# Depthwise 7x7 filter as band-matrix products: blocks of 4 full-width rows become blocks of 7 half-width rows

## The chip, the cores and the metric

The kernel runs on one core of a Trainium2 chip. The metric is the device time of one execution in microseconds (us); lower is better. The kernel before takes 3096.03 us (median of 3 runs, 3095.71 to 3096.39). PE is the matrix engine (its weight loads are shown as PEld), DVE the vector engine, ACT the scalar engine, POOL the general engine, SP the engine that issues most DMAs.

## What is computed

A batch of 32 images of 384 channels and 28 x 28 pixels goes through one ConvNeXt block and a gate. Cut to what matters:

```
y = conv(x, dw_w, padding 3, feature_group_count=C) + dw_b    # 7x7, one filter per channel
y = (y - mean_c) * rsqrt(var_c + eps) * ln_g + ln_b            # over the channels
y = gelu(y @ w1 + b1)                                          # 384 -> 1536
y = grn_g * (y * gx / (mean(gx) + eps)) + grn_b + y            # gx = norm over the pixels
z = x + (y @ w2 + b2)                                          # 1536 -> 384
out = sigmoid(logits(mean, max, min of z) + z)
```

The change bears on the first line. All data are fp32.

## The kernel before

There are two stages. The first, some 0.5 ms, computes the depthwise filter for all images, channel by channel; the second runs image by image through the two large products (`up` and `down`), each computed with fewer block products by a scheme of sums (`UPSTEPS`, `STEPS`, `SUMS`).

**The filter as matrix products.** An image is cut into NJ = 7 blocks of RW = 4 rows. A row is padded to a pitch PW = 32, so that a block is a vector of 4 x 32 = 128 numbers, which lie on the 128 partitions. Each channel has a band matrix (each column is the filter's weights, shifted by one). A block of the output is the sum of three products: the block itself, the block after and the block before, each with another 128 (or 96) columns of the band matrix. All blocks of all 32 images stand side by side as moving columns: 7 x 32 = 224 for the block itself (L599), 6 x 32 = 192 for each neighbour (L601, L603), since the outermost blocks have one neighbour only. So a channel has three products. A product in fp32 appears in the profile as two records, one for each of two passes; a transpose has one.

**The steps.** `for s in range(NK)` has 48 steps of TC = 8 channels. `conv(s, c2, ...)` does two channels into one PSUM tile `pc` (four tiles rotate), and the result, with the bias, is copied into `yc`: even pairs by two ACT activations (L615), odd pairs by one DVE addition (L607). `yc` holds 16 channels for all images; `store` sends it to DRAM (`yd`, and the last two groups to `yl`).

**Band matrices.** `sequences(cb)` puts the 49 weights of a channel into a row of zeros of FL = 355 numbers, which is written to DRAM (`fs`). `load_t(s)` reads a step's matrices back into `tmat` with one DMA, in which every partition reads the same row shifted by one number (128 partitions, 11,360 bytes each). It is issued three steps ahead.

**The input.** `load_x` fetches a tile of XC = 32 channels by 4 images (128 partitions, 784 pixels). `pad_x` copies it into the pitch of 32 (`xpad`, three rotate; POOL for the first chunk of 32 channels, ACT after that, L448). `turn_x` transposes it on PE, block by block, in two halves of 4 and 3 blocks (L460, seven transposes a tile), and copies the result into `xt` (DVE, L469). `spread` deals this work for the next chunk out among the pairs of the current one: `plan` sets behind which pair each half tile goes, and `pad_next(i + 1)` stands ahead of the first half of tile i. PE executes in the written order (`keep`).

**SP's queue** carries, in written order: `load_t`, `load_x`, the stores of `yc`, and the stores of the combined weight blocks `u` that POOL forms meanwhile (`form_w`).

**The end of the first stage.** The last 16 channels are done twice with half of the images each (`B0 = 16`): first images 0 to 15, then 16 to 31. With the first half done, image 0 has all its channels, and `first_image` (normalisation, transposes back to channel order, sums of `forms_up`) is dealt out among the pairs of the second half. Then `up(0)` begins.

**The second stage.** For each image `load_y` fetches the filter's result, DVE computes statistics per block (`block_stats`), ACT normalises per block (`norm`, 384 numbers a pixel), PE transposes three times per block (`turn`, L816), ACT copies into `room` and leaves the padding out (`untwist`, called by `evac`), and POOL forms the sums. Where these stand among the products is written by hand in `within` and `beside`. There are 7 blocks an image, hence 21 transposes.

Of the kernel before, what the change touches and what calls it, by code (L numbers as in the profile page):

```python
# [21 lines left out]
RH = HW // 2  # L22
# [7 lines left out]
RW = 4  # L30
NJ = HW // RW
PW = P // RW
XC = 32
# [3 lines left out]
REACH = 3 * PW  # L37
MW = P + 2 * REACH
T0 = P - REACH

SN = 6 * PW + 7
S0 = T0 + REACH + P - 1 - 3 * PW - 3
FL = S0 + SN
NLAST = XC // YC
# [149 lines left out]
def convnext_gate_kernel(  # L196
# [15 lines left out]
    N = NJ * B  # L212
# [5 lines left out]
    fs = [dram.tile([P + 1, FL], F32, name=f"fs_{cb}") for cb in range(CB)]  # L218
# [60 lines left out]
    def stats(b):  # L279

        mv = sts[b] = smp.tile([P, NJ, 2], F32, tag="mv", name=f"mv_{b}")
        if b == 0:
            bs = bss[0].rearrange("p j i v -> p j (i v)")
        else:
            bs = bss.pop(b)
        for j in range(NJ):
            nc.vector.bn_aggr(mv[:, j, :], bs[:, j, :])
# [6 lines left out]
    def std(b):  # L294
        mv = sts[b]
        sd = smp.tile([P, NJ], F32, tag="sd", name=f"sd_{b}")
        nc.scalar.activation(sd, mv[:, :, 1], AF.Sqrt, bias=eps_t, scale=1.0)
        rstd = smp.tile([P, NJ], F32, tag="rstd", name=f"rstd_{b}")
        nc.vector.reciprocal(rstd, sd)
        nmr = smp.tile([P, NJ], F32, tag="nmr", name=f"nmr_{b}")  # L300
        nc.vector.scalar_tensor_tensor(nmr, mv[:, :, 0], -1.0, rstd, ALU.mult, ALU.mult)
        sts[b] = rstd, nmr
# [7 lines left out]
    def untwist(eng, acc, cb, j0, j1, pt):  # L310

        affine(
            eng,
            acc[:, cb, j0 * RW * HW : j1 * RW * HW].rearrange("p (r w) -> p r w", w=HW),
            pt[:, : j1 - j0, ::-1].rearrange("p j (r w) -> p j r w", w=PW)[:, :, :, :HW],
            lng_t[:, cb : cb + 1],
            lnb_t[:, cb : cb + 1],
        )
# [28 lines left out]
    with ExitStack() as one:  # L347
# [28 lines left out]
        tab = ws[:, : CB * FL].rearrange("p (cb m) -> p cb m", m=FL)  # L376
# [10 lines left out]
        nc.vector.memset(tab, 0.0)  # L387

        def sequences(cb):
            nc.vector.tensor_copy(  # L390
                tab[:, cb, S0 : S0 + SN - 7].rearrange("p (y x) -> p y x", x=PW)[:, :, :7],
                dww[:, cb, :42].rearrange("p (y x) -> p y x", x=7),
            )
            nc.vector.tensor_copy(tab[:, cb, S0 + SN - 7 :], dww[:, cb, 42:])
            return nc.scalar.dma_start(fs[cb][:P, :], tab[:, cb, :])

        sequences(0)
        zrow = scratch([FL], 1)
# [3 lines left out]
        def load_t(s, parts=1):  # L402
            base = fs[s * TC // P]
            n = TC // parts
            for i in range(parts):
                nc.sync.dma_start(
                    tmat[s % NT2][:, i * n : (i + 1) * n, :].rearrange("p c m -> p (c m)"),
                    bass.AP(
                        tensor=base.tensor,
                        offset=base.offset + (s * TC % P + i * n) * FL,  # L410
                        ap=[[1, P], [1, n * FL]],
                    ),
                )
# [3 lines left out]
        xpad = [tp.tile([P, HW, PW], F32, name=f"xpad_{i}") for i in range(NPAD)]  # L417
        for t in xpad:
            nc.gpsimd.memset(t[:, :, HW:], 0.0)
# [21 lines left out]

        def pad_x(i):
            dst = xpad[i % NPAD][:, :, :HW]
            src = xis.pop(i).rearrange("p (r w) -> p r w", w=HW)
            if i < NG:
                nc.gpsimd.tensor_copy(dst, src)
            else:
                nc.scalar.activation(dst, src, AF.Identity)  # L448
# [3 lines left out]
        def turn_x(i, h, xt, eng=nc.vector):  # L452

            g = i % NG
            xv = xt.rearrange("p c (j b) -> p j c b", j=NJ)
            j0, j1 = 4 * h, min(NJ, 4 * h + 4)
            pt = psx.tile([P, 4, P], F32, tag="pt", name=f"pt_{i}_{h}")
            for j in range(j0, j1):
                keep(
                    nc.tensor.transpose(  # L460
                        pt[:, j - j0, :],
                        xpad[i % NPAD][:, j * RW : (j + 1) * RW, :].rearrange("p r w -> p (r w)"),
# [3 lines left out]
            dst = xv[:, j0:j1, :, g * NB : (g + 1) * NB]  # L466
            src = pt[:, : j1 - j0, :].rearrange("p j (c q) -> p j c q", q=NB)
            if eng is nc.vector:
                eng.tensor_copy(dst, src)  # L469
            else:  # L470
                eng.activation(dst, src, AF.Identity)  # L471
# [57 lines left out]
        AHEAD = NG  # L529

        def pad_next(i):
            if i < GT:
                pad_x(i)
                if i + AHEAD < GT:
                    load_x(i + AHEAD)

        for i in range(AHEAD):
            load_x(i)
        xt = new_xt(0)
        for i in range(NG):  # L540
# [4 lines left out]
            if i == NG - 2:  # L545
                for cb in range(CB):
                    if cb:
                        keep(sequences(cb))
                    keep(nc.scalar.dma_start(fs[cb][P:, :], zrow))
            if i == NG - 2:  # L550

                nc.gpsimd.tensor_copy(tmat[1][:, 0, :1], xpad[i % NPAD][:, 0, :1])
                load_t(1)
            if i + AHEAD < GT:
                load_x(i + AHEAD)
            for h in range(2):
                turn_x(i, h, xt, (nc.vector, nc.scalar)[h])
        pad_next(NG)

        later = {  # L560
# [4 lines left out]
            U2 - 3: (  # L565
                ws.rearrange("p (fb c) -> p fb c", c=C),
                w2.rearrange("(fb p) c -> p fb c", p=P),
            ),
# [9 lines left out]
        B0 = min(B, 16)  # L578

        def conv(s, c2, yc, xt, b0, b1):  # L580

            t = tmat[s % NT2]
            nb = b1 - b0
            if not nb:
                return
            pc = psc.tile([P, 2, 256], F32, tag="pc", name=f"pc_{s}_{c2}_{b0}")
            for ci in range(2):
                c = 2 * c2 + ci
                if nb == B:
                    po = pc[:, ci, :N]  # L590
                    xc = xt[:, s % SK * TC + c, :]
                    after, before = xc[:, B:], xc[:, : N - B]
                    lo, hi = po[:REACH, : N - B], po[:, B:]
                else:
                    po = pc[:, ci, : NJ * nb].rearrange("p (j b) -> p j b", b=nb)
                    xc = xt[:, s % SK * TC + c, :].rearrange("p (j b) -> p j b", b=B)[:, :, b0:b1]
                    after, before = xc[:, 1:], xc[:, : NJ - 1]
                    lo, hi = po[:REACH, : NJ - 1], po[:, 1:]
                keep(nc.tensor.matmul(po, t[:, c, P : 2 * P], xc, start=True, stop=False))  # L599
                keep(  # L600
                    nc.tensor.matmul(lo, t[:, c, 2 * P : T0 + MW], after, start=False, stop=False)  # L601
                )
                keep(nc.tensor.matmul(hi, t[:, c, :P], before, start=False, stop=True))  # L603
            cc = s * TC + 2 * c2
            cy = cc % YC
            if c2 % 2:
                nc.vector.tensor_tensor(  # L607
                    yc[:, b0:b1, :, cy : cy + 2].rearrange("p b j c -> p c j b"),
                    pc[:, :, : NJ * nb].rearrange("p c (j b) -> p c j b", j=NJ),
                    dwb[:, cc : cc + 2].unsqueeze(2).unsqueeze(3).to_broadcast([P, 2, NJ, nb]),  # L610
                    ALU.add,
                )
            else:
                for ci in range(2):
                    nc.scalar.activation(  # L615
                        yc[:, b0:b1, :, cy + ci].rearrange("p b j -> p j b"),
                        pc[:, ci, : NJ * nb].rearrange("p (j b) -> p j b", j=NJ),
# [5 lines left out]
        def store(yc, kt, b0, b1):  # L623
# [6 lines left out]
            if b0 == 0:  # L630
                for j in range(NJ):
                    nc.vector.bn_stats(bss[0][:, j, 2 + i, :], yc[:, 0, j, :])
                nc.vector.tensor_copy(yis[0][:, kt], yc[:, 0])
            (nc.sync if b1 < B or i + 1 < NLAST else nc.scalar).dma_start(
                yl[:, i, b0:b1], yv[:, b0:b1]
            )
# [16 lines left out]
        def first_image(n):  # L653

            V, A = nc.vector, nc.scalar
# [12 lines left out]
            elif n in (2, 3):  # L668
                h = n - 2
                j0, j1 = 4 * h, min(NJ, 4 * h + 4)  # L670
# [10 lines left out]
                for cb in range(CB):  # L681
                    untwist((A, V, A)[cb], room_acc, cb, j0, j1, py[cb])
# [3 lines left out]
        for s in range(NK):  # L686
            k, si = divmod(s, SK)
            if s + 3 < NK:
                if s == 0:
                    for i in range(2, 4):  # L690
                        nc.gpsimd.tensor_copy(tmat[i][:, 0, :1], xpad[i % NPAD][:, 0, :1])
# [17 lines left out]
            if s >= NK - 2:  # L709


                if s == NK - 1:
                    for n in range(2 * PAIRS):
                        conv(NK - 2 + n // PAIRS, n % PAIRS, yc, xt, 0, B0)
                    store(yc, kt, 0, B0)
                    for i in range(0, NS, UG):
                        for t in range(2):
                            first_u1[t, i] = load_u1(t, i)
                    for n in range(2 * PAIRS):
                        conv(NK - 2 + n // PAIRS, n % PAIRS, yc, xt, B0, B)  # L720
                        first_image(n)
                    if B0 < B:
                        store(yc, kt, B0, B)
            else:
                for c2 in range(PAIRS):
                    conv(s, c2, yc, xt, 0, B)
                    if k + 1 < NX:
                        spread(k + 1, si * PAIRS + c2, xn)
                if s % 2:
                    store(yc, kt, 0, B)  # L730

                    for h, (k0, k1) in enumerate(((0, NY - NLAST - 4), (NY - NLAST - 4, NY - NLAST))):
                        if kt != k1 - 1:
# [476 lines left out]
```

## Time and profile before

| what | us |
|---|---|
| median of the runs | 3096.03 |
| time of the profiled execution | 3095.95 |
| its span, first to last instruction | 3094.2 |
| first product of the filter starts | 20.46 |
| last step with all images together ends | 471.9 |
| first product of `up(0)` starts | 496.04 |
| transposes of the input, L460 | 672, of which 56 ahead of the first product |
| transposes back in the second stage, L816 | 31 images x 21 |

The profile is of one execution. "Busy" is the time in which an engine had at least one instruction under way; matmuls overlap one another, so the mean duration of a record is longer than the time from one start to the next. In a list of instructions, "x2" means that two records were merged into one line; a duration is then that of both together. In the chain of waits each line gives start, duration and the instruction that the end of the run goes back to. A group line gives busy time, mean duration of one and the idle time of the engine just before it, with what ended it.

### The profile page before, as it was taken

Reading aid. Unit: us, or ns where it says so; the run is one execution under the profiler, and the core shown is the slowest. Engines: PE = TensorE matmul, PEld = TensorE weight load, DVE = VectorE, ACT = ScalarE, POOL = GpSimd, SP = SyncE. Lnnn points to the kernel's source line nnn. Section 1 sums busy time; section 2 is a strip of 40 time slices with the busy share of each in tenths; the row PEclk is TensorE's granted clock in tenths of the full one; section 3 lists DMA queues with packets and bytes.
Section 4 is the critical chain, followed back from the end, with each engine's and each line's share of the span. In section 5 each row is a group of like instructions: output and inputs, shape, how many; then the busy total and the mean of one; then the engine's idle time right before and its main releaser. Section 6 shows DMA issues by size and latency. Waiting matters only on the chain.

```text
span 3094.2 us, 45727 instructions
## 1 busy us (share of the span) xinstructions
PE 3059.3 (99%) x15011; PEld 2486.7 (80%) x15011; DVE 1986.1 (64%) x5378; ACT 1986.7 (64%) x3151; POOL 2263.1 (73%) x1767
## 2 busy tenths in 40 slices
PE   8999999999999999999999999999999999999997
PEld 8999997777777777777777777777777777777777
DVE  3444446666667777776667667666666666666665
ACT  3333335757777777777777777777777777777771
POOL 1233442798888888888888888888888888888887
PEclk9999999999999999999999999999999999999999
DMA  9999987455555655556656565655556555555545
GB/s 369 362 373 350 355 326 230 138 157 190 190 189 191 190 190 190 191 191 192 197 189 197 189 197 190 196 193 187 185 182 197 183 182 186 187 190 190 190 152 188
DMA packets 316132, 658.31 MB, mean 213 GB/s; under 512 B 127583, under 2 KB 142202, under 8 KB 306938
## 3 DMA queue, kind: packets, MB, share of 16 engines
q1 hardware_dynamic: 302916, 616.59, 60.2%
q10 hardware_dynamic: 12982, 38.80, 3.2%
q8 instruction: 122, 2.00, 0.3%
q14 instruction: 112, 0.92, 0.1%
HBM read 560.78 MB, written 94.53 MB: 212 GB/s over the span
## 4 chain that ended last, share of the span: by engine, by line
PE 95%; POOL 3%; ACT 1%; DVE 1%; DMA 1%; issue 0%; ACTq 0%; SPq 0%; POOLq 0%; DVEq 0%
PE ph_A L858 13%; PE ph_C L858 13%; PE ph_B L858 13%; PE pz_A L980 8%; PE pz_C L980 8%; PE pz_D L980 7%; PE pz_F L980 7%; PE pc L599 5%; PE pc L603 4%; PE pc L601 4%; PE py L816 2%; PE pt L460 2%; PE pz_H L980 2%; PE pz_E L980 2%; PE pz_I L980 2%; POOL d_room L941 1%
## 5 line engine op out<-in xcount | busy, mean ns | idle before, releaser
L941 POOL TENSOR_TENSOR d_room<-y 128x588 f32<-128x588 f32 x257 | 368.2, 1439 | 342.4 <-PE pz_B L980 194.0
L308 ACT ACTIVATE y<-y,fv,gsc 128x784 f32<-128x784 f32 x376 | 362.8, 1031 | 378.6 <-DVE gsc L894 378.6
L828 ACT ACTIVATE y<-y,fv 128x784 f32<-128x784 f32 x384 | 350.1, 945 | 186.4 <-DVE y L873 164.4
L858 PE MATMUL ph_A<-room,ws 128*128 128x392 f32 x1240 | 461.3, 494 | 0.8 <-ACT te L865 0.4
L858 PE MATMUL ph_C<-room,ws 128*128 128x392 f32 x1240 | 462.0, 495 | 0.0
L858 PE MATMUL ph_B<-room,ws 128*128 128x392 f32 x1240 | 458.8, 492 | 1.3 <-DVE yc L607 1.3
L941 POOL TENSOR_TENSOR d_room<-d_room,y 128x588 f32<-128x588 f32 x309 | 442.5, 1436 | 16.8
L858 PEld LDWEIGHTS ph_C<-room,ws 128*128 128x128 f32 x1240 | 233.1, 190 | 179.6 <-DVE y L871 20.6
L858 PEld LDWEIGHTS ph_A<-room,ws 128*128 128x128 f32 x1240 | 233.1, 190 | 178.7 <-ACT te L865 13.3
L858 PEld LDWEIGHTS ph_B<-room,ws 128*128 128x128 f32 x1240 | 234.8, 190 | 164.7 <-issue 1.5
L941 POOL TENSOR_TENSOR d_room<-y,d_room 128x588 f32<-128x588 f32 x220 | 316.0, 1437 | 46.0 <-PE pz_A L980 18.2
L834 ACT ACTIVATE junk<-y 128x784 f32<-128x784 f32 x384 | 329.0, 857 | 8.1
L343 POOL TENSOR_TENSOR room<-room 128x392 f32<-128x392 f32 x300 | 300.4, 1018 | 11.8
L941 POOL TENSOR_TENSOR y<-y 128x588 f32<-128x588 f32 x188 | 269.7, 1435 | 7.3
L867 DVE TENSOR_TENSOR y<-y,ph_C 128x392 f32<-128x392 f32 x384 | 214.3, 559 | 27.4
L1002 DVE TENSOR_REDUCE stq<-x 128x1 f32<-128x196 f32 x768 | 228.2, 349 | 5.5
L869 DVE TENSOR_TENSOR y<-y,ph_B 128x392 f32<-128x392 f32 x256 | 137.4, 557 | 143.5 <-ACT y L828 119.4
L615 ACT ACTIVATE yc<-pc,dwb 128x224 f32<-128x224 f32 (+1 forms) x200 | 103.5, 619 | 192.6 <-PE pc L603 184.1
L599 PE MATMUL pc<-xt,tmat 128*128 128x224 f32 (+1 forms) x800 | 213.9, 349 | 5.6 <-ACT xt L471 4.1
L980 PE MATMUL pz_A<-d_room,u 128*128 128x196 f32 x1056 | 204.9, 330 | 0.0
L524 POOL TENSOR_SCALAR u<-ws 128x384 f32<-128x384 f32 (+1 forms) x53 | 66.5, 1259 | 186.7 <-DMA u2d<-u 133.8
L469 DVE COPY xt<-pt 128x512 f32<-128x512 f32 (+1 forms) x184 | 112.1, 619 | 135.0 <-PE pt L460 135.0
(219 smaller groups left out, 6619.2 us busy)
## 6 DMA issues: line engine op xcount, KB each, us to landing
u<-u2d SPq DMA_DIRECT2D x487, 384.0 KB, 3.4
ws<-u1d SPq DMA_DIRECT2D x384, 320.0 KB, 3.0
tmat<-fs SPq DMA_DIRECT2D x47, 1420.0 KB, 11.4
ws<-u2d SPq DMA_DIRECT2D x121, 384.0 KB, 3.2
yd<-yc SPq DMA_DIRECT2D x22, 1792.0 KB, 6.6
yi<-yd SPq DMA_DIRECT2D x31, 1232.0 KB, 8.0
x<-in_x SPq DMA_DIRECT2D x32, 1176.0 KB, 5.4
out<-x ACTq DMA_DIRECT2D x31, 1176.0 KB, 7.2
```

The costliest lines, as they stand in the source:

```text
L308: eng.activation(out, in_, AF.Identity, bias=add, scale=mul)
L343: tc.keep_in_program_order(eng.tensor_tensor(d, o[in0], o[in1], op))
L599: keep(nc.tensor.matmul(po, t[:, c, P : 2 * P], xc, start=True, stop=False))
L601: nc.tensor.matmul(lo, t[:, c, 2 * P : T0 + MW], after, start=False, stop=False)
L828: nc.scalar.activation(y, y, AF.Gelu, bias=b1_t[:, f : f + 1], scale=1.0)
L834: nc.scalar.activation(junk, ys[b][:, f, :], AF.Square, accum_out=ssqs[b][:, f : f + 1])
L858: nc.tensor.matmul(banks[t, bk][:, :NH], wts[t][:, i % UG, :], o[opnd], start=(first == 1), stop=True, skip_group_check=True,)
L867: nc.vector.tensor_tensor(d, d, p, ALU.add)
L869: nc.vector.tensor_tensor(d, d, p, ALU.subtract)
L941: nc.gpsimd.tensor_tensor(d[0], o[a][0], o[c][0], ALU.add if sign == "+" else ALU.subtract)
L980: nc.tensor.matmul(pz[:, :NQ4], wt[:, i % UD, t, :], o[opnd][0][:, t, :], start=(first and t == 0), stop=(t == KD - 1), skip_group_check=True,
L1002: nc.vector.tensor_reduce(stq[:, v, m, h : h + 1], xh, AX.X, op2)
```

## The change

The blocks become 7 rows high and half as wide. The output of a block has 7 x 14 pixels in a pitch of PR = 19 (the last row is not padded, so 6 x 19 + 14 = 128 output partitions). The input blocks have 7 rows and KW = 18 columns (14, 3 of a neighbour and 1 over), 126 partitions, with the row index fastest, and are offset by 3 rows against the output: an output block needs two input blocks, the one above (`up_`) and the one below (`down_`). There are NV = 4 output blocks and NI = 5 input blocks per half, so NJ = 8 blocks an image, and per channel two halves x two products, all with 128 weight columns and 4 x 32 = 128 moving columns.

- A chunk has XC = 16 channels (two steps of 8) by 8 images instead of 32 by 4; there are still 96 tiles, now with eight transposes each.
- `pad_x` has four copies instead of one, since it also turns row and column over; the fifth block is made of three rows at the end and four at the start, and `turn_x` puts it to both ends with a mask (`ends`): three copies a half tile instead of one.
- FL is 268 instead of 355. `fs` has three variants per channel (all weights; first column alone; last column alone, for the outermost input columns), and `load_t` has three DMAs: 112 partitions, 7 and 7.
- The split of the last 16 channels is gone. `first_image` stands behind the last product, behind 36 transposes of the identity (`NWARM`) that no one reads.
- In the second stage an image has 8 blocks: 24 transposes, 8 normalisations and statistics. `yd` grows by 8/7. Several small tiles have two buffers instead of three. The load of `w2` is in two halves.

The core of the diff:

```diff
-RW = 4
-NJ = HW // RW
-PW = P // RW
-XC = 32
+RW = 7
+OW = HW // 2
+KW = OW + 4
+PR = OW + 5
+KP = RW * KW
+NV = HW // RW
+NJ = 2 * NV
+NI = NV + 1
+XC = 16
...
-                keep(nc.tensor.matmul(po, t[:, c, P : 2 * P], xc, start=True, stop=False))
-                keep(
-                    nc.tensor.matmul(lo, t[:, c, 2 * P : T0 + MW], after, start=False, stop=False)
-                )
-                keep(nc.tensor.matmul(hi, t[:, c, :P], before, start=False, stop=True))
+                for h, up_, down_ in ((0, UP_L, DOWN_L), (1, UP_R, DOWN_R)):
+                    po = pc[:, ci, h * NV * B : (h + 1) * NV * B]
+                    xc = xt[:KP, s % SK * TC + c, h * NI * B : (h + 1) * NI * B]
+                    for n, (m0, j) in enumerate(((up_, 1), (down_, 0))):
+                        keep(
+                            nc.tensor.matmul(
+                                po, t[:KP, c, m0 : m0 + P], xc[:, j * B : (j + NV) * B],
+                                start=(n == 0), stop=(n == 1),
+                            )
+                        )
...
+                for v, e0, ne in ((0, 1, KW - 2), (1, 0, 1), (2, KW - 1, 1)):
+                    nc.sync.dma_start(
+                        t[e0 * RW : (e0 + ne) * RW],
+                        bass.AP(
+                            tensor=base.tensor,
+                            offset=start + v * (P + 1) * FL + e0,
+                            ap=[[1, ne], [PR, RW], [1, n * FL]],
+                        ),
+                    )
...
+            d, x0 = xpad[i % NPAD], xis.pop(i)
+            xw = x0.rearrange("p (r w) -> p w r", w=HW)
+            for h, e0, c0 in ((0, 1, 0), (1, 0, HW - KW + 1)):
+                dst = d[:, h, : NV - 1, e0 : e0 + KW - 1, :]
+                src = xw[:, c0 : c0 + KW - 1, RW - 3 : HW - 3]
+                copy((A, V, G)[h + 1 if i < NG else 0], dst, src.rearrange("p w (j r) -> p j w r", r=RW))
...
+            copies = [(xv[:, 1:NV], src[:, : NV - 1], None)]
+            for v, j in enumerate((NV, 0)):
+                copies.append((xv[:, j], src[:, NV - 1], ends[:KP, v : v + 1]))
...
-                if s == NK - 1:
-                    for n in range(2 * PAIRS):
-                        conv(NK - 2 + n // PAIRS, n % PAIRS, yc, xt, 0, B0)
-                    store(yc, kt, 0, B0)
...
-                    for n in range(2 * PAIRS):
-                        conv(NK - 2 + n // PAIRS, n % PAIRS, yc, xt, B0, B)
-                        first_image(n)
...
+            if s == NK - 1:
...
+                for n in range(NWARM):
+                    pw = psx.tile([P, 4, P], F32, tag="pt", name=f"pw_{n}")
+                    for j in range(4):
+                        keep(nc.tensor.transpose(pw[:, j, :], ident, ident))
+                for n in range(4):
+                    first_image(n)
...
-            for i, jj in ((0, (0, 1)), (3, (2, 3)), (7, (4, 5)), (TURNED, (6,))):
+            for i, jj in ((0, (0, 1)), (3, (2, 3)), (7, (4, 5)), (TURNED, (6, 7))):
```

## The prediction

> **What bounds the kernel.** I read the page first, then the busy times by stage, the groups of the filter stage with shapes kept apart, the instructions of PEld, and the chain of waits at the seam of the two stages.
>
> ```profile
> PE 3059.3 (99%) x15011; PEld 2486.7 (80%) x15011; DVE 1986.1 (64%) x5378; ACT 1986.7 (64%) x3151; POOL 2263.1 (73%) x1767
> ...
> PE 95%; POOL 3%; ACT 1%; DVE 1%; DMA 1%; issue 0%; ACTq 0%; SPq 0%; POOLq 0%; DVEq 0%
> ```
> ```profile
> 20.00:460.00 440.00, 438.02 (x2758) 424.64 (x2759) 181.64 (x280) 162.47 (x268) 154.00 (x146) 0.99 0.94 358
> 460.00:496.00 36.00, 34.56 (x284) 33.94 (x282) 18.40 (x59) 13.16 (x30) 10.42 (x10) 1.00 0.79 266
> ...
> 600.00:3000.00 2400.00, 2397.41 (x11091) 1879.75 (x11092) 1657.36 (x4672) 1699.25 (x2667) 1969.63 (x1501) 1.00 0.58 187
> ```
>
> (Stretch, length, then PE, PEld, DVE, ACT, POOL busy, clock, DMA share, GB/s.) PE is the bound in both stages, at full clock: the time is a count of PE passes times their spacing, plus the seam. In the filter stage weight loads are nearly as busy as products, and DMA is at 0.94, close behind. DVE, ACT and POOL have more than half of that stage to spare.
>
> ```profile
> L599 PE MATMUL pc<-xt,tmat 128*128 128x224 f32 x736 | 201.1, 355 | 5.6 <-ACT xt L471 4.1 <-issue 1.5
> L601 PE MATMUL pc<-xt,tmat 128*96 128x192 f32 x736 | 180.6, 327 | 0.0
> L603 PE MATMUL pc<-xt,tmat 128*128 128x192 f32 x736 | 180.6, 327 | 0.0
> ...
> L460 PE MATMUL pt<-ident,xpad 128*128 128x128 f32 x672 | 102.4, 278 | 7.2 <-POOL xpad L446 7.1
> ```
>
> 736 records are 368 channels x 2 passes. The means are latencies; the spacing must come from starts. In the chain, L601 of successive channels starts at 460.09 and, 11 channels on, at 471.40 us: 1.028 us a channel, or 608 moving columns x 2 passes at 0.846 ns. It is the moving columns that cost.
>
> The new passes have only 128 moving columns, and the weights still 128. What a pass costs once the moving side is that short is shown by the last 16 channels, which run with half of the images (112, 96, 96 columns). Weight loads there:
>
> ```profile
> 474.29 0.30 PEld L599 LDWEIGHTS pc<-xt,tmat 128*128 128x128 f32 x2
> 474.51 0.26 PEld L601 LDWEIGHTS pc<-xt,tmat 128*96 128x96 f32 x2
> 474.69 0.30 PEld L603 LDWEIGHTS pc<-xt,tmat 128*128 128x128 f32 x2
> 474.91 0.30 PEld L599 LDWEIGHTS pc<-xt,tmat 128*128 128x128 f32 x2
> ...
> 484.95 0.30 PEld L599 LDWEIGHTS pc<-xt,tmat 128*128 128x128 f32 x2
> ```
>
> 17 channels from 474.29 to 484.95: 0.627 us a channel, where 304 columns x 2 at 0.846 ns would be 0.514. So here the loads set the pace: two loads of 128 weight columns take 0.223 us (474.69 to 474.91), **0.1115 us a pass**, whatever moves.
>
> **The change, part by part.**
>
> *Products of 46 steps.* 368 channels go from 1.028 us to 4 products x 2 passes. Bounds of a pass: 128 moving columns x 0.846 ns = 0.108 us below; 0.191 us above, the mean record of a 128-column fp32 load (it would hold if such loads could not overlap each other). A transpose has the new shape, 128 weights by 128 columns: six of L816 in 0.82 us, the last 0.273 long, make (0.82 - 0.273) / 5 = 0.109.
>
> ```profile
> 1070.02 0.82 PE L816 MATMUL py<-ident,yn 128*128 128x128 f32 x6
> ```
>
> I take 0.1115, the row with fp32 weights in two passes: 8 x 0.1115 = 0.892 us, 368 x (0.892 - 1.028) = **-50.0 us**.
>
> [...]
>
> *The last 16 channels.* Twice 0.627 becomes 0.892: 16 x (0.892 - 1.254) = **-5.8 us**.
>
> *Transposes of the input.* 96 tiles x 8 instead of x 7; ahead of the first product there are now 4 tiles x 8 = 32 instead of 56. On the path 736 instead of 616: 120 x 0.109 = **+13.1 us**.
>
> *Seam.*
>
> ```profile
> 481.84 0.24 PE pc L603 x2
> 482.10 0.56 DVE yc L607
> 482.75 0.63 DVE bs L632 x7
> 483.50 0.91 DVE mv L287 x7
> 484.44 0.31 ACT sd L297
> ...
> 485.98 1.53 PE py L678 x12
> ...
> 488.73 0.98 PE py L678 x9
> ...
> 496.04 1.55 PE ph_B L858 x4
> ```
>
> Before, image 0's normalisation ran beside the second half of the products. From 471.89 to 496.04 are 24.15 us; 16 x 1.254 = 20.06 of it are products, so 4.1 us are not covered. Now the chain stands bare. From the last product: 0.2 to the DVE copy, 1.05 for it (512 numbers; 931 ns for 448), 0.76 statistics of 8 blocks (0.67 for 7), 1.13 aggregation (0.99 for 7), 0.85 root, reciprocal and shift (484.41 to 485.25 without the copy between), 1.9 to the end of the first 12 transposes (485.44 to 487.4, for 4 blocks), 1.9 for two ACT copies of 0.65 and the DVE one (three PSUM tiles, so the second 12 transposes wait for them), 1.2 for these, 1.3 for their copies, 0.55 for the first sum on DVE and 0.2: 11.0 us. The next operands need q, r, s and then five more sums at 0.55 each while PE has 1.32 us of work a pair: some 1.5 us of waits. 12.5 - 4.1 = **+8.4 us**. The 36 idle transposes (3.9 us) end before the real ones begin, so they cost nothing; without that cover, 3.9. `up(0)` also holds a bn_stats (546 ns), an aggregation and a DVE norm more for image 1, where DVE is full from 505 to 515 us: **+1**.
>
> *Second stage.* 31 images x 3 transposes x 0.109 = **+10.1 us**, in the open, since PE is busy 2397 of 2400 us. ACT gains a norm of 695 ns an image; it idles 0.29 of the stage. The new eighth norm follows the copies that end at 1077.7 us in one image, its transposes stand after 1081.9: 3.6 us of slack. `yi` grows from 1232 to 1408 KB under a DMA share of 0.58. Nothing for these, nor for fewer buffers of tiles that live less than two images.
>
> *Feeding the new stage.* A step is 8 x 0.892 + 16 x 0.109 = 8.9 us. ACT: four copies of 256 numbers at 0.63 x 256/224 = 0.72, and two tiles of 952 numbers, bounded by 1.10 ns a number (L448, 862 ns for 784) and 2.83 (L615, 634 ns for 224, strided): 5.0 to 8.3 us. DVE: two additions of 1.06, and four half tiles of 548 ns plus two masked copies of 0.21 (72 numbers) to 0.55 (384): 6.0 to 8.7. Both fit. Behind a pair's ACT copy stands the pad of tile 1, which PE wants 0.88 + 1.78 us later; 0.2 + 1.15 + 1.1 to 1.7 us on ACT leaves between 0.2 of slack and 0.4 of wait, over 23 chunks 0 to 9 us. SP gets two more issues of 0.32 to 2.15 us a step; it now waits some 250 us of 440 for compute. I take **+3** for such waits, between 0 and 20.
>
> *Start.* The table write is larger (412 against 182 KB), fewer tiles come first. Bounds -4.3 us (PEld's wait for ACT ahead of the first product) and +6.65 (the write of fs again); I take **0**, as the two oppose each other.
>
> **Sum:** -50.0 - 5.8 + 13.1 + 8.4 + 1 + 10.1 + 3 + 0 = -20.2. The profiled execution took 3095.95 us (span 3094.2 and 1.75 around it), 0.08 below the median: 3075.7, so **3076 us**.
>
> **Rivals.**
>
> *Loads do not keep pace (slower).* In the conv loop every pass becomes load-bound, with no long product behind which a load could hide. 3072 passes decide: from 0.1115 + 20.2/3072 = 0.118 us a pass on, all is lost. At 0.143, the record of a transpose's load, it is 3072 x 0.0315 = 97 us more: 3173 us. Against it: both short-pass rows lie at 0.109 to 0.1115. For it: neither row has all passes at 128 by 128 in fp32.
>
> *DMA takes over.* The stretch from 20 to 460 us moved 158 MB; 46 steps of tmat at 1.08 instead of 1.45 MB and 22 stores 0.26 MB larger leave 146 MB, for 409 us of PE. At 358/0.94 = 381 GB/s that is 383 us, hidden; at 342 GB/s, the lowest 40 us at a share of 0.95, 427 us: +18, 3094 us, no change. For it: a spare of only 26 us, three DMAs where one was.
>
> [...]
>
> *Cheaper than thought.* Pass at 0.108 (-10.8) and no new waits (-3): 3062 us.
>
> **Chances.** Forecast 0.55 (own range 3064 to 3090), DMA 0.17, loads 0.15, cheaper 0.13. A measurement can tell 0.2%, 6 us, from no change. Faster takes the cheaper case, nearly all of the forecast and a little of DMA: 0.68; within 0.2%: 0.12; slower: loads and the rest of DMA: 0.20. The range is 3058 (cheaper, and part of the start's gain) to 3104 (DMA and 10 us of waits together); most of the loads case stays outside.
>
> **What would show it.** Loads of `pc` spaced 0.1115 us; the last product near 446 us instead of 494; `up(0)` starting some 11 us later; 24 transposes an image and each image 0.33 us longer; L460 768 times. Wrong if the spacing exceeds 0.118, if PE's idle time before `pc` or `pt` goes to DMA or ACT with more than 20 us, or if the second stage grows by more than its transposes.

## Result and profile after

The changed kernel takes 3147.42 us (median of 4 runs, 3145.94 to 3151.96), beside 3095.87 (3094.62 to 3096.39) for the kernel before: ratio 1.017, 95% interval 1.0152 to 1.0187. It is slower, where 3076 us and faster were forecast. The profiled execution took 3145.94 us, its span is 3144.2.

Three parts of the page of the changed kernel: busy times, the 40 slices (DMA share, GB/s), and the shares of the chain that ended last.

```profile
PE 3048.0 (97%) x15913; PEld 2490.0 (79%) x15913; DVE 2059.3 (65%) x5833; ACT 2146.3 (68%) x3458; POOL 2265.0 (72%) x1776
...
DMA  9999999455665666566656566555555566656545
GB/s 257 277 321 308 316 307 322 149 167 190 196 197 191 194 197 195 191 196 197 190 190 189 187 196 192 187 188 187 189 190 189 189 192 193 191 190 192 192 153 187
...
PE 76%; DMA 16%; POOL 3%; DVE 3%; issue 1%; ACT 0%; SPq 0%; ACTq 0%; POOLq 0%; DVEq 0%
```

DMA's share of the chain went from 1 to 16%, and PE has idle time again. Where, the groups say (last two numbers: idle time before the group, and who ended most of it):

```profile
L653 PE MATMUL pc<-xt,tmat 126*128 126x128 f32 x3072 | 385.9, 283 | 55.1 <-DMA tmat<-fs 53.3
```

PE waits 53.3 us for band matrices. ACT waits for input tiles (58.1 us, "DMA room<-in_x", ahead of its copies into `xpad`); PE in turn waits 5.8 us for ACT. The same 300 us of the filter stage, in the kernel before and then in the changed one (columns as in the stretches of the prediction):

```profile
100.00:400.00 300.00, 298.49 (x1896) 289.46 (x1895) 124.63 (x191) 111.39 (x184) 115.76 (x105) 1.00 0.96 366
```
```profile
100.00:400.00 300.00, 268.75 (x2261) 264.83 (x2259) 173.77 (x404) 189.47 (x340) 103.34 (x94) 0.95 1.00 310
```

DMA's share rose to 1.00 while its rate fell from 366 to 310 GB/s. The share is the time that packets took; so the packets became slower (an input row took 193 ns instead of 133, in the table below). PE stood idle for 31 us of 300, and the mean granted clock fell to 0.95. After a stall the first products run slower (15 passes in 3.11 us, in the last line of the timeline further down, where 16 take 1.95 ahead of it).

SP's queue tells the same (us in total, times, longest). Before, it waited for compute; now it waits for earlier transfers to land. Before, then changed:

```profile
SPq L627 <- DVE yc L607: 141.2, 20, 11.1
SPq L406 <- PE pt L460: 41.1, 17, 6.3
```
```profile
SPq L423 <- DMA tmat<-fs: 98.3, 49, 3.9
SPq L796 <- DMA yd<-yc: 39.2, 9, 4.9
SPq L465 <- DMA yd<-yc: 20.9, 7, 4.5
```

In both traces the transfers issued by SP and ACT (1,361 before, 1,459 in the changed kernel) tell of their landing by eight semaphores, each used 170 or 171 times before and 182 or 183 times now, and a semaphore is used again only when the transfer before on it has landed: at no time are more than eight under way. From 100 to 400 us there were 153 transfers for 32 steps' matrix loads before, 4.8 a step, and 197 for 29 now, 6.8 a step.

The trace has a record of each DMA packet. In the filter stage their sizes tell what they carry: 3136 B is an input row, 8576 B (before 11,360) a row of matrices, 16,384 B (before 14,336) a piece of a store. Sorted by size, from 100 to 400 us (sums of bytes and of durations; the kernels named e are the experiments below):

| kernel | time, us | input row, ns | matrix row, B/ns | store, B/ns | GB/s |
|---|---|---|---|---|---|
| before | 3096 | 133 | 24.9 | 26.0 | 365 |
| changed | 3147 | 193 | 18.6 | 25.8 | 304 |
| e1, no edge loads | 3115 | 193 | 18.1 | 26.0 | 315 |
| e4, one load a step | 3113 | 188 | 20.7 | 26.0 | 330 |
| e6, input rows in sequence | 3145 | 184 | 18.7 | 25.9 | 306 |
| e8, three even loads | 3167 | 209 | 16.5 | 25.9 | 292 |
| e18, three even loads, input rows in sequence | 3147 | 181 | 15.9 | 26.0 | 304 |
| e10, nearly no matrices | 3105 | 177 | none | 24.5 | 249 |
| e13, one load, input rows in sequence | 3069 | 127 | 24.2 | 26.1 | 378 |

Reads from DRAM slowed by a quarter to a third in the changed kernel; stores did not. (Time counts here from the first packet, 11 us ahead of the first instruction, so the rates differ a little from those of the stretches.)

### The profile page after: what moved, and what is told of

Same layout as the page of the kernel before. It is cut to its first block, busy times and chain, and to the rows that moved or that the text cites. A ratio compares the mean times of both kernels' runs of the same rounds, so it can differ in the third digit from the quotient of the medians.

```text
span 3144.2 us, 48626 instructions
## 1 busy us (share of the span) xinstructions
PE 3048.0 (97%) x15913; PEld 2490.0 (79%) x15913; DVE 2059.3 (65%) x5833; ACT 2146.3 (68%) x3458; POOL 2265.0 (72%) x1776
## 4 chain that ended last, share of the span: by engine, by line
PE 76%; DMA 16%; POOL 3%; DVE 3%; issue 1%; ACT 0%; SPq 0%; ACTq 0%; POOLq 0%; DVEq 0%
PE ph_C L901 12%; PE ph_B L901 12%; PE ph_A L901 12%; DMA tmat<-fs 8%; PE pz_A L1023 7%; PE pz_C L1023 7%; PE pz_D L1023 7%; PE pz_F L1023 6%; DMA yi<-yd 3%; PE py L859 2%; PE pc L653 2%; PE pz_E L1023 2%; DMA room<-in_x 2%; PE pz_H L1023 2%; DMA yd<-yc 2%; POOL d_room L984 2%
## 5 line engine op out<-in xcount | busy, mean ns | idle before, releaser
L653 PE MATMUL pc<-xt,tmat 126*128 126x128 f32 x3072 | 385.9, 283 | 55.1 <-DMA tmat<-fs 53.3
L653 PEld LDWEIGHTS pc<-xt,tmat 126*128 126x128 f32 x3072 | 370.2, 198 | 61.2 <-issue 49.3
L478 ACT ACTIVATE xpad<-room 128x357 f32<-128x357 f32 (+2 forms) x320 | 188.1, 631 | 115.6 <-DMA room<-in_x 58.1
```

Source lines behind the costliest of these rows:

```text
L653: nc.tensor.matmul(po, t[:KP, c, m0 : m0 + P], xc[:, j * B : (j + NV) * B], start=(n == 0), stop=(n == 1),)
```

## The experiments

The first theory: the two loads of 7 partitions, with their small size, take places among the eight transfers under way, or, being only 7 packets of 8,576 B each, load a few engines, so that DMA falls behind. (No trace tells which engine carried a packet; how a load is shared out is the author's estimate throughout.) Rivals: the pattern in which a matrix's rows are read (steps of 19 numbers), the pitch of the larger store, the new order of the input (16 channels by 8 images). Each kernel ran once, beside the kernel before on the same chip (3093.1 to 3096.3 us, so chips differ by up to 3 us); differences below some 9 us, 0.3%, are not read; the four runs of the changed kernel lie within 6.0.

**e1: without the two edge loads.**
```diff
-                for v, e0, ne in ((0, 1, KW - 2), (1, 0, 1), (2, KW - 1, 1)):
+                for v, e0, ne in ((0, 1, KW - 2),):
```


> Leaves out the two loads of 7 rows per step (the matrices' first and last input columns stay zero), so each step has one load of 112 rows; all else as changed. Theory 'few engines': the 7-row loads lie on the same few DMA engines, which hold up the rest; without them the waits of the products for tmat (53 us) and most of the rest of the filter stage's excess go: about 3065 to 3080 us. Theory 'three issues': SP's queue is slowed by two more issues a step; same number. Theory 'row pattern': the rows of 19 numbers' stride are read slowly from DRAM; the big load stays, so about 3135 to 3147. Theory 'input or stores': nothing moves, 3147.

3114.7 us: 33 us come back; 39 more are missing to the forecast's 3076. PE still waits 22.6 us for matrices. There is a second cause.

**e2: the edge loads from ACT's queue.**
```diff
-                    nc.sync.dma_start(
+                    (nc.scalar if v else nc.sync).dma_start(
```


> The two 7-row loads of a step are issued on ACT's queue instead of SP's. Few engines: unchanged, 3140 to 3155. Three issues: SP is free of them, about 3070 to 3095. Row pattern, input or stores: unchanged, 3147.

3206.3 us. The load's wait now stands in ACT's own queue, ahead of its copies. Waits of e2:

```profile
ACT yc L669 <- DMA tmat<-fs: 72.0, 12, 13.5
PE pt L516 <- ACT xpad L478: 68.2, 15, 12.2
```

**e3: rows shifted by one number, as before, still three loads.**
```diff
-                            ap=[[1, ne], [PR, RW], [1, n * FL]],
+                            ap=[[1, ne * RW], [1, n * FL]],
```


> The three loads stay, but each row is read one number further on than the row before (as in the kernel before) instead of in steps of 19 numbers; the filter's values are then others. Row pattern: the waits go, 3065 to 3085. Few engines and three issues: unchanged, 3140 to 3155.

3148.6 us: no difference. With one load a step it makes none either (e1 keeps the steps of 19, e4 below does not). It was not tried with the input in another order.

**e4: one load of 128 rows a step, as in the kernel before.**
```diff
+                nc.sync.dma_start(
+                    t,
+                    bass.AP(tensor=base.tensor, offset=start, ap=[[1, P], [1, n * FL]]),
+                )
```


> One load a step of all 128 rows, each one number further on, as in the kernel before but with rows of 8.6 KB; the filter's values are then others. Few engines, three issues and row pattern all say 3065 to 3080. Input or stores (the tile of 16 channels by 8 images, the larger yc): 3140 or more, since nothing of theirs is changed.

3112.8 us, as e1, though it moves more bytes. Dropping the small loads is worth some 35 us; their bytes are not the cost.

**e5: a pad behind each partition's part of the store** (pitch of 33 images instead of 32).
```diff
-    yd = dram.tile([P, NY - NLAST, B, NJ * YC], F32, name="yd")
+    yd = dram.tile([P, NY - NLAST, B + 1, NJ * YC], F32, name="yd")
```


> The filter's result in DRAM gets a place for a 33rd image that is never written, so that a partition's row of 16 channels is 16,896 bytes apart from the next instead of 16,384 (before the change: 14,336). Theory 'pitch': stores at a pitch of a power of two are slow and hold up the other transfers; with the pad DMA moves more than 340 GB/s at a full share instead of 300 to 320, and about 30 to 40 us go: 3105 to 3120. Theory 'input': the stores are innocent, 3140 to 3152.

3158.8 us: 11 us slower, no gain. Neighbouring partitions of `yd` lie 22 pieces of 16,384 bytes apart, 360,448 bytes (with the pad 371,712), which is no power of two in either case. **e12** is the same pad on e4:

> e4 (one load of 128 rows a step; other values) with the padded pitch of the stores alone. If the stores at 16,384 bytes' pitch are what slowed e4 against e11, this ends at 3075 to 3085 as e11 did and the stores land in some 8 us; if the input's 8 images are, 3105 to 3118.

3131.1 us, 18 slower than e4. The pitch of the stores is out, as the table's store column says too.

**e6: the input's rows in sequence, alone** (128 rows of DRAM that follow one another make a tile).
```diff
-            base = x[g * NB, k * XC : k * XC + 1, :]
+            base = x[g * NB, k % 16 * XC : k % 16 * XC + 1, :]
...
-                    ap=[[NT, XC], [C * NT, NB], [1, NT]],
+                    ap=[[NT, P], [1, NT]],
```


> Each tile of the input is fetched as 128 rows that follow one another in DRAM (other channels of fewer images, so other values) instead of 16 channels of 8 images; bytes and rows are the same. Theory 'input' (8 images at a distance of 1.2 MB read more slowly than 4): 3105 to 3120. Theory 'pitch': 3140 to 3152.

3145.0 us: no difference while the three loads are there. The edit changes more than the order: the tiles of one group of images now overlap, so that only 1,472 different rows of the input's 12,288 are read, each about eight times.

**e7: the small loads as 16 rows of 3.8 KB.**
```diff
+                    m = n * FL * RW // 16
+                        t[:16, (v - 1) * m : v * m],
...
+                            ap=[[1, 16], [1, m]],
```


> The two small loads of a step stay two, with the same bytes, but go to 16 rows of 3.8 KB instead of 7 of 8.6 KB (other values in the matrices). Theory 'few engines': they are spread evenly, and the 33 us that leaving them out gained are gained here too: 3110 to 3122. Theory 'three issues': the number of loads is what costs, 3140 to 3152.

3201.7 us, but this answers another question: the small loads write partitions of the large one, so they wait for it to land. SP's waits of e7:

```profile
SPq L433 <- DMA tmat<-fs: 274.8, 40, 10.6
```

**e8: three loads of 96, 16 and 16 rows,** each a multiple of 16.
```diff
+                for p0, np_ in ((16, 96), (0, 16), (112, 16)):
...
+                            ap=[[1, np_], [1, n * FL]],
```


> Three loads of matrices a step as in the changed kernel, but of 96, 16 and 16 rows of 8.6 KB (each row one number further on; other values), so that every load can be dealt evenly to 16 engines; 1.10 MB instead of 1.08. Theory 'few engines': the 33 us of the 7-row loads go, 3108 to 3120. Theory 'window of eight' (in the program a DMA is issued only when the one eight before it has landed, so two more DMAs a step leave fewer bytes under way): unchanged, 3140 to 3155.

3167.4 us. The same bytes as e4, cut in three, cost 54.6 us more, with the same input as in the changed kernel. That an edge load is only 7 packets is not it. A stretch of e4, then of e8:

```profile
200.00:300.00 100.00, 90.91 (x785) 89.89 (x783) 60.03 (x142) 65.98 (x120) 25.29 (x24) 0.97 1.01 322
```
```profile
200.00:300.00 100.00, 81.28 (x676) 79.80 (x675) 51.22 (x119) 56.30 (x101) 28.77 (x25) 0.94 1.03 301
```

**e9: e1 and two loads of 16 bytes a step.**
```diff
+            for _ in range(2):
+                nc.sync.dma_start(tiny[ntiny[0] % 16][:1], cvec[0:1, :4])
```


> One load of 112 rows a step as in e1, and two loads of 16 bytes each to a tile that no one reads. Window of eight: the two take their places in the window without moving bytes, so the 33 us come back, 3138 to 3155. Few engines: almost nothing is added to any engine, 3110 to 3122.

3124.5 us, 10 above e1, hardly more than a single run can tell. Two more places taken among the eight explain about a third of the 33 us here. That may be too little: the 16-byte packets end some 7 us (median) after their issue, while the 16-row loads of e8 land after 11.6, so the tiny loads hold their places for less time.

**e10: matrices for the first four steps only.**
```diff
+            if s >= NT2:
+                return
```


> Matrices are loaded for the first four steps only and used again after that (other values). If DMA alone separates the result from the forecast, the filter stage now runs at its passes: last product at 440 to 455 us and 3065 to 3080 us in all. If something else does (ACT's four pads, DVE's three copies, the clock), 3095 or more.

3104.7 us. Not the forecast's time, since another wait took over: in SP's queue the stores of `yc` now stand behind those of `u`, which wait for POOL, and ACT waits for the room. SP's waits, then those of the engines:

```profile
SPq L798 <- POOL u L589: 87.5, 28, 8.2
```
```profile
ACT yc L671 <- DMA yd<-yc: 62.9, 7, 18.3
```

Its packets say more than its time: with no matrix load beside them, input rows still take 177 ns, against 133 before, where a tile was 32 channels by 4 images. Both kernels read every row once. That points at the order of 16 channels by 8 images itself.

**e11 and e13: e4 with the input's rows in sequence,** e11 with the pad too. Edit as in e6.

> e4 (one load of 128 rows) with both the tile of input from consecutive rows and the padded pitch of the stores (other values). In e4 and e1 DMA still moved only some 325 GB/s at a full share, against 360 at 0.94 before. If the input's 8 images or the stores' pitch cause that, it moves 350 or more and ends at 3075 to 3095; if they don't, 3105 to 3118.

> e4 (one load of 128 rows a step) with the input from consecutive rows alone (other values). If the input slowed e4, 3075 to 3085; if the stores' pitch did, 3105 to 3118.

3078.3 and 3069.2 us: both faster than the kernel before (by 15 and 24 us on their chip). The edit of the input is worth 43.6 us on e4, and nothing on the changed kernel (e6). A stretch and one of SP's waits of e13:

```profile
100.00:400.00 300.00, 300.00 (x2698) 299.80 (x2697) 211.35 (x492) 225.76 (x406) 131.57 (x122) 1.00 0.99 379
```
```profile
SPq L674 <- DVE yc L654: 140.0, 21, 9.6
```

PE never stops, at full clock; DMA is at 379 GB/s at the same share; SP waits for compute again, as before the change. So neither edit alone brings this, and both together do. How much of the 43.6 us is the order, and how much the repeated reading of few rows, these runs do not separate.

**e14: the edge loads from POOL,** and the pad.
```diff
+                    (nc.gpsimd if v else nc.sync).dma_start(
```


> [...] Few engines or mere traffic: 3140 or more. POOL's own work could hold the loads up; then the products wait for tmat more than 53 us.

3172.5 us. The loads now have a queue of their own (q0, 3.19 MB from 100 to 400 us), but POOL stands idle for 99.2 us ahead of them, waiting for free room. Waits of e14:

```profile
POOL tmat L423 <- PE pc L653: 99.2, 14, 24.9
```

**e15 and e16: the image as the outer index of an input tile,** the same 128 rows; e15 on e4, e16 on the changed kernel, with matrices of 16 channels in each load.
```diff
-                    ap=[[NT, XC], [C * NT, NB], [1, NT]],
+                    ap=[[C * NT, NB], [NT, XC], [1, NT]],
```


> One load of 128 rows a step, as in e4 (3112.8 us; it leaves out the zeros' variants of the two outer columns), and the input tile of 16 channels by 8 images read with the image as the outer index, so that one queue entry's neighbouring partitions are 16 consecutive rows (50 KB) of one image. The same rows are read as in the changed kernel. If it is the order in which the rows stand that was slow in e4, this reaches e13 (3069) within some 6 us, with PE busy throughout from 100 to 400 us and DMA at 380 GB/s. If the 8 images of a tile, far apart in DRAM, are what is slow, or if e13 was quick because it reads other rows, it stays near 3113.

> The changed kernel whole, with the same work, the input read as in e15, and the matrices loaded for 16 channels at a time: three loads for two steps instead of three for each, the same bytes, two tiles of 16 channels instead of four of 8. If the number of loads (with their landing times under a limit on transfers in flight) and the input's order are the two causes, DMA keeps pace again and it lands between 3069 and 3085, faster than both kernels. If loads on 7 partitions are slow for another reason than their number, it stays above 3110.

3206.0 and 3249.8 us, the worst but for no reason that was expected. A stretch of e15:

```profile
100.00:400.00 300.00, 250.25 (x2057) 246.28 (x2056) 156.44 (x371) 170.91 (x311) 81.73 (x75) 0.93 0.82 281
```

DMA's share itself fell to 0.82. With the image outside, the outermost size is 8, and hardly ever were more than eight input packets under way at once: at the middle of 98% of them eight or fewer were, against 50% in e4. That the outermost size sets this number is the author's estimate from these packets. Both runs are confounded by it.

**e17: tiles of 8 channels by 16 images** (outermost size 16, 8 neighbouring rows each), and edge loads of 16 channels at a time, on the changed kernel: two loads of matrices a step instead of three.
```diff
+                    ap=[[C * NT, XI], [NT, XH], [1, NT]],
...
+                if s % 2 == 0:
+                    load_t(s + 2, 0, 2 * TC, EDGES)
```


> The changed kernel whole, the same work. An input tile is 8 channels of 16 images instead of 16 of 8, with the image as the outer index: the outermost size is 16 again (e15 and e16 had 8 there, and DMA's share fell to 0.76 to 0.84), and behind each image are 8 consecutive rows (25 KB). The two loads of 7 partitions fetch 16 channels at a time, so there are two loads of matrices a step instead of three, with the same bytes. If the slow order of the input and the number of small loads are the two causes, it lands between 3069 and 3095, as e13 did (3069) with a single load. If the bytes on 7 partitions are what costs, whatever their number, it stays between 3110 and 3150. If the outermost size of 8 was not what slowed e15, the tile of 16 images does no better and DMA's share stays below 0.9.

3179.5 us: 32 slower than the changed kernel, where 50 to 80 faster was expected. DMA's share is back near 1 (0.96 to 1.02 in six stretches), which agrees with the outermost size as e15's trouble. But input rows take 197 ns: half as many small loads, with tiles of 8 neighbours of 16 images, is not enough. Two things changed at once here, so neither is priced.

**e18: e8 with the input's rows in sequence.**

> e8 (the 128 rows of the matrices in three loads of 96, 16 and 16, so that all 16 engines have the same work; 3167) with the input tiles read as 128 rows that follow one another, as in e13 (3069, one load) and e6 (3145, loads of 112, 7 and 7). It leaves out the zeros' variants of the two outer columns and reads other input rows. If what costs 76 us between e13 and e6 is that the small loads keep only 7 of the 16 engines busy and set the engines apart, this is as quick as e13, 3069 to 3080, with row packets of the input near 127 ns. If it is the number of loads, it is near e6, 3125 to 3150, with these packets near 185 ns.

3146.6 us, 77 above e13, from which it differs only in the cut of one load into three. Loads of 96, 16 and 16 rows do no better than loads of 112, 7 and 7 (e6: 3145.0). A stretch of e18:

```profile
100.00:400.00 300.00, 262.36 (x2206) 257.99 (x2207) 168.86 (x396) 185.04 (x330) 103.39 (x94) 0.95 1.03 307
```

## Why the prediction was wrong

**Right: what PE has to do.** In the changed kernel, where nothing is late, 16 passes take 1.79 us, 0.112 a pass (forecast 0.1115), here from 200.12 to the transposes at 201.91:

```profile
200.12 1.95 PE L653 MATMUL pc<-xt,tmat 126*128 126x128 f32 x16
201.91 0.60 PE L516 MATMUL pt<-ident,xpad 128*126 128x128 f32 x4
202.35 1.95 PE L653 MATMUL pc<-xt,tmat 126*128 126x128 f32 x16
204.13 0.60 PE L516 MATMUL pt<-ident,xpad 128*126 128x128 f32 x4
...
209.25 3.11 PE L653 MATMUL pc<-xt,tmat 126*128 126x128 f32 x15 [1.85 <-DMA tmat<-fs]
```

Four transposes take 0.44 us (0.11 each; forecast 0.109). The rival of load-bound passes falls with this. Loads and products overlap: one after the other, by an estimate from the prediction's 0.1115 and 0.108, they would take some 0.22 us a pass, and from 100 to 400 us PE was busy 268.75 us and PEld 264.83. In e13, with DMA out of the way, the last product ends at 451.9 us. The three terms -50.0, -5.8 and +13.1 make 451 out of the 494 of before (the 446 in the prediction's list does not follow from its own terms); e13's first product starts 4.1 us earlier than before, and PE waits 7.5 us for ACT's copies into `xt`, so these terms hold within some 4 us. The whole takes 23.8 us less than the kernel before on that chip (forecast -20.2), though e13 leaves out the edge matrices and reads other input.

**Right: the seam, nearly right: the second stage.** Chain of the changed kernel (start, duration, what):

```profile
510.31 17.88 PE pc L653 x160
...
532.04 2.50 ACT xt L315 x4
535.17 1.55 PE py L728 x12
...
538.49 2.46 PE ph_B L901 x6
```

From the end of the products, 528.2, to the first product of `up(0)`, 538.5, are 10.3 us; 11.0 had been worked out. `up(0)` itself grew by 1.7 us (forecast 1, and 1.5 of waits at its start). From image 0's product `pg` to the last image's, the second stage grew from 2452.4 to 2458.0 us, by 5.6, where +10.1 had been put for 93 transposes in the open. The transposes did cost what was said: 98.2 us busy for 720 in that stretch against 88.4 for 630. The same number of products took less (into `ph_A` 444.0 against 446.3, into `ph_C` 444.8 against 446.9); why is not shown. The start came 2.8 us earlier (first product at 17.69), inside its bounds around 0.

**Wrong: "Feeding the new stage", +3, between 0 and 20.** It counted ACT's and DVE's work, which does fit (e13), and gave SP's two more issues their issue time only. The last product ends near 528 us instead of the 451 that the terms make, so this step cost 77 us. Its cover was the working of the rival "DMA takes over": 146 MB at 381 GB/s, 383 us, hidden under 409 us of PE. The rival had the right mechanism in kind and the right reason for it (a spare of 26 us, three DMAs where one was), and the wrong size: it bounded the rate by the slowest 40 us of the kernel before, 342 GB/s, so +18 us. But that rate belongs to that kernel's transfers. The bytes were right, 147 MB from 20 us to 506, when the last matrices had landed. The rate was 303 GB/s, and with it the rival's own division gives 146 MB / 303 GB/s = 482 us, 73 beyond PE's 409. Seen from PE, here are the stretches from the first to the last product, the changed kernel and then e13:

```profile
17.69:528.18 510.49, 451.20 (x3813) 444.85 (x3814) 290.09 (x681) 315.09 (x566) 165.04 (x156) 0.95 0.99 303
```
```profile
16.36:451.93 435.57, 428.08 (x3813) 427.60 (x3814) 289.97 (x681) 313.51 (x566) 165.06 (x156) 0.99 0.95 359
```

For the same records of PE, the changed kernel takes 74.9 us more: 51.8 of them idle, and 23.1 in which PE is busy longer, at the lower clock and after the stalls.

**What lowered the rate.** The edge loads' 7 packets are not it: loads of 96, 16 and 16 rows cost as much (e18 against e6, 3146.6 and 3145.0 us). Cutting a step's matrix load in three is one cause, and it was shown twice: +55 us with the changed kernel's input (e8 against e4), +77 us with the input's rows in sequence (e18 against e13). The order of 16 channels by 8 images in a tile is probably the other: input rows take 188 ns in e4 and 177 in e10, against 133 before, and all three kernels read each row once. What it costs is not shown, since the 44 us between e4 and e13 also hold the repeated reading of few rows. The changed kernel is 78 us slower than e13, not the sum of 77 and 44: with only one of the two edits the reads stay at 16 to 21 bytes per ns (e4, e6), where e13 has 24 to 25.

**Left open.** Why a load cut in three is read more slowly, row by row, is not settled. Places among the eight transfers under way explain some 10 us (e9); whether they explain more with loads of full size was not separated. The matrix rows do come apart in time: before, at the middle of 84% of matrix packets 13 or more of them were under way at once, in the changed kernel at 14%, in e13 at 55%; but e18, with 53%, is slow. Also open is what makes 16 neighbouring rows of 8 images a slow order, when 32 of 4 was quick. e13 reads few rows many times and has no edge matrices, so it shows what the stage could take, not a kernel to use; of the kernels that do the whole work none beat the kernel before.

## What to carry to other kernels

The DMA rate taken from the profile held for the transfers that made it (381 GB/s had been counted on, 303 came): where a change cuts a load in several or reads rows in another order, price the stage at a lower rate too, and ask how much spare there is before anything else. A DMA share of 1.0 did not say that DMA delivered what it could (310 GB/s at 1.00 in the changed kernel, 379 at 0.99 in e13); read GB/s beside it, and the duration of packets of one size. And test suspected causes of slow loads in pairs: here one of two edits gained 35 us alone, the other nothing, and both together 78 us. An edit that is to change only an order must also leave what is read as it was.

## What was not expected of the hardware

- The same 128 rows of matrices, read by three loads instead of one, took 540 ns a row instead of 355 (e18, e13), with stores at 26.0 and 26.1 bytes per ns.
- While no input packet was under way, e4's matrix rows came at 24.5 bytes per ns; with 5 to 8 of them under way, at 18.0. In e13, whose input tiles are rows in sequence, many of them read again and again, it made no such difference (23.5 and 25.7).
- Stores in pieces of 16,384 B, neighbouring partitions 22 such pieces apart, were not slow: a pad of 512 B behind each made no kernel quicker (9 to 18 us slower in one run each: e11 against e13, e5, e12).
- With an outermost size of 8 in the input tile, DMA's share fell from 1.01 to 0.82 (e4, e15, from 100 to 400 us), and the time rose by 93 us.
